# Due times of the last eight chunks, and issue and landing costs of transfers by their kind, in the planner of a two-layer transformer kernel

## The chip, the core and the metric

The kernel runs on one core of one Trainium2 chip. The metric is the device time of one execution in microseconds (us), smaller is better. A core has five engines with a queue each: PE (TensorE, the matrix engine), DVE (VectorE), ACT (ScalarE), POOL (GpSimd) and SP (SyncE), which here issues every DMA. Each engine works off its queue in order, so the order in which instructions are issued decides who waits for whom.

## The reference

The input is x of 8 sequences with 1024 rows of 256 numbers, all float32. Four blocks follow each other, each with a layernorm before it and a residual sum after it:

```python
x = x + decoder(_layernorm(x), ...)      # flow attention, 16 heads of 16; own residual, layernorms and
                                         # a feed-forward 256 -> 1024 -> 256 with gelu
x = x + relu(_layernorm(x) @ w1 + b1) @ w2 + b2          # 256 -> 1024 -> 256
t = _layernorm(x)                        # softmax attention over the whole sequence, one head of 256
Q, K, V = split(t @ W_qkv.T + b_qkv)
x = x + softmax(Q @ K.T / 16) @ V
t = fp4(_layernorm(x))                   # fp4: blocks of 16, scale = max/6, rounded to 8 magnitudes
x = x + fp4(silu(t @ fp4(w_gate).T) * (t @ fp4(w_up).T)) @ fp4(w_down).T     # 256 -> 704 -> 256
```

The flow attention is causal (running sums along the sequence). The softmax attention isn't: a row needs the keys of its whole sequence.

## The kernel before

Rows are handled in chunks of 128 (64 in all, 8 in each sequence) and in groups p of four chunks (16 in all, two in each sequence). `linear_attention` does the flow attention group by group, `dense` the two feed-forward layers, for which it streams the weights from HBM again for every group (`w_in`, `w_out`, tiles of 128 KB, five buffers each), `norms_1` and `norms_2` the layernorms between. `soft_chunk(cc)` does softmax attention and the fp4 layer for chunk cc (0 to 63): `n2T,wqk` (the query), four products `n2T,qT` (scores), `ident,prob` or `ident,flow` (transposes of the probabilities), `vt,probT`, then layernorm and fp4 rounding on DVE, `ident,n` (transposes), two pairs of `wgT,xqT` and `wuT,xqT`, SiLU and product into a tile of 704 columns (`hid`, or `q` and `k` where free buffers of those names are lent), the fp4 rounding of it on DVE with one square on ACT, `ident,hid` (transposes), `wdT,hqT`, the last sum `y` and the store.

The order of all this isn't written out by hand. While the program is built, every part is a Python generator that yields what its next step needs, and `Plan.run` picks among them. For that, `Plan.took` keeps a cost model of each queue: a cost by engine, operation and size, and, for a DMA, when it lands. `Plan.run` takes the step with the smallest key:

```python
key = wait, unripe, queue == "tensor", not stays, part[2]
```

`part[2]` is the due time `at`. It decides last, among steps that are as ready as each other. Due times are counted in groups: group p of the flow attention is due from p, `dense` from p + 1 to p + 2, chunk cc of `soft_chunk` from 3.5 + cc/4, with its transposes 0.25, 0.5 and 0.75 later. A chunk starts when its whole sequence is normed and fewer than eight chunks are in flight; at most three are between their scores and their `vt,probT` product.

When the model sees TensorE idle for more than 1.6 us, and a bank of PSUM is free, `Plan.run` calls `fill`, which puts products of the identity with itself (`bank<-ident`) into the gap, 0.22 us of them at a time, for the length of the gap less 0.7 us. One such product is two passes in the trace. Nothing reads them.

In the flow attention `spread` widens a small tile: two DMAs write `packed` (128 x 128) to HBM, then four (`flow`) or two (`scale`) read it back as `spread` tiles of 128 x 512. For every transfer the model had one cost, and one time to landing beyond that of its bytes:

```python
        else:
            cost = 0.4
...
            after = self.free["rings"] - end + 2.1
```

Every instruction goes through `Queue.issue` (the helper's line, L337 in the profile), so groups of instructions are told apart by their tiles and not by their lines.

Of the kernel before, what the change touches and what calls it, by code (L numbers as in the profile page):

```python
# [16 lines left out]
P = 128  # L17
# [45 lines left out]
class Plan:  # L63
# [96 lines left out]
    def took(self, queue, op, args, kw):  # L160

        aps = [x for x in list(args) + list(kw.values()) if isinstance(x, bass.AP)]
        outs = [kw["out"] if "out" in kw else aps[0]]
        if kw.get("accum_out") is not None:
            outs.append(kw["accum_out"])
        size = 1
        for ap in aps:
            n = 1
            for d in ap.shape[1:]:
                n *= d  # L170
            size = max(size, n)

        overlap, after = 0.0, 0.035
        if queue == "tensor":
            size = 1
            for d in outs[0].shape[1:]:
                size *= d
            cost = size * (0.853e-3 if op == "transpose" else 1.687e-3)
            tiled = op == "matmul" and (kw["lhsT"].shape[-1] <= 32 or kw["lhsT"].shape[0] <= 32)
            if tiled or op == "matmul" and kw["lhsT"].dtype == BF16:  # L180
                cost *= 0.25
            if tiled != self.tiled:
                cost += 0.2
            self.tiled = tiled
            after = 0.2
        elif queue == "vector":
            each = {"reciprocal": 6.2e-3, "tensor_tensor_scan": 2.15e-3}.get(op, 1.05e-3)
            cost = 0.17 + each * size
            if op == "tensor_scalar" and outs[0].dtype == BF16:
                cost = 0.16 + 0.26e-3 * size  # L190
            elif op == "scalar_tensor_tensor" and any(ap.shape[-1] == 1 for ap in aps):
                cost += 0.06
            overlap = 0.08
        elif queue == "scalar":
            cost = (0.16 if op == "copy" else 0.26) + 0.82e-3 * size
            for x in args:
                if not isinstance(x, bass.AP) and self.SETS.get(x, self.act_set) != self.act_set:
                    self.act_set = self.SETS[x]
                    self.free[queue] = self.free.get(queue, 0.0) + 1.3
            if kw.get("accum_out") is not None:  # L200
                cost += 0.15
            overlap = 0.1
        elif queue == "gpsimd":
            cost = 0.65 + 0.7e-3 * size
            if op in ("tensor_scalar", "iota"):
                cost = 0.22
            elif op == "memset":
                cost = 0.1 + 0.9e-3 * size
        else:
            cost = 0.4  # L210
        start = self.free.get(queue, 0.0)
        if queue not in ("tensor", "sync"):
            start = max([start] + [self.used.get(ap.tensor.name, 0.0) for ap in outs])
        for ap in aps:
            name = ap.tensor.name
            if self.by.get(name) != queue or queue in ("vector", "gpsimd"):
                start = max(start, self.done.get(name, 0.0) + (0.05 if queue == "gpsimd" else 0.0))
            if name not in self.done and name in self.held:
                start = max(start, self.used[name])
        if queue == "tensor":  # L220
            if start - self.ran > 2.0:
                self.slow = start + 2.1
            if start < self.slow:
                cost *= 2
            self.ran = start + cost
        if queue == "sync":
            start = max(start, self.landed.pop(0))
        end = start + cost
        if queue == "sync":
            n = 4e-6 / 250e-3  # L230
            for d in outs[0].shape:
                n *= d
            self.free["rings"] = max(self.free.get("rings", 0.0), end) + n
            after = self.free["rings"] - end + 2.1
            self.landed.append(end + after)
        self.free[queue] = end - overlap
        for ap in outs:
            self.done[ap.tensor.name] = end + after
            self.by[ap.tensor.name] = queue
        for ap in aps:  # L240
            name = ap.tensor.name
            self.used[name] = max(self.used.get(name, 0.0), end + after)
            if queue != "tensor" and name not in self.kept:
                self.held.discard(name)
# [11 lines left out]
    def pe(self, *tiles, **kw):  # L256
        return self.need("tensor", tiles, **kw)

    def dve(self, *tiles, **kw):
        return self.need("vector", tiles, **kw)  # L260
# [95 lines left out]
def block_stack_kernel(ctx: ExitStack, tc: tile.TileContext, a: dict, out: bass.AP):  # L356
# [20 lines left out]
    plan = Plan(tc, tc.nc)  # L377
    nc, pe, dve, act, dma = plan, plan.pe, plan.dve, plan.act, plan.dma
    x_dram = a["L0_attn_inputs"]
    B, L, _ = x_dram.shape  # L380
    NCH = L // P
# [1120 lines left out]
    def soft_chunk(cc):  # L1502
# [1 line left out]
        g, i = divmod(c, G)  # L1504
        q = seqs[s]
        n2T, vt = q["n2T"], q["vt"]
        at = 3.5 + cc / 4
        yield pe(
            banks=1,
            when=lambda: count["asked"] == cc  # L1510
# [130 lines left out]
    def softmax_and_fp4():  # L1641
        for cc in range(B * NCH):
            q = seqs[cc // NCH]
            yield dve(
                at=3.5 + cc / 4,
                when=lambda: q["normed"] == NCH and cc - count["out"] < (8 if plan.spare else 4) and "softmax" in weights and "ends" in late,
            )
            plan.start(soft_chunk(cc), 3.5 + cc / 4)

    def fill(us):  # L1650

# [7 lines left out]
    for part in (linear_attention(), masks(), late_constants(), zeros(), load_weights_and_rows(), dense(), softmax_and_fp4(), fp4_weights(), softmax_weights()):  # L1659
        plan.start(part, 0.0)  # L1660
# [43 lines left out]
```

## Time and profile before

| | |
|---|---|
| median of 3 runs | 2649.98 us (2648.61 to 2650.44) |
| the profiled execution's own time | 2649.28 us |
| its span, first to last instruction | 2647.6 us |
| mean granted TensorE clock | 0.999 |
| PE, DVE, ACT, POOL busy | 2610.0, 1927.3, 1308.1, 576.9 us |
| transfers of `w_in` and `w_out` | 1024 of 128 KB |
| transfers of `packed`, `spread` | 60 of 64 KB, 90 of 256 KB |

The profile is of one execution. Its own time is 1.68 us longer than its span and 0.70 us under the median of the runs. A line of a timeline has the start, the time, the engine, the operation, the tiles out<-in, the shape and the count, and in brackets the idle time before it with what ended it. A line of windows has the stretch, its length, and the busy time of each engine in it (with the count of instructions), then the granted TensorE clock, the share of DMA and GB/s.

### The profile page before, as it was taken

Reading aid. Unit: us, or ns where it says so; the run is one execution under the profiler, and the core shown is the slowest. Engines: PE = TensorE matmul, PEld = TensorE weight load, DVE = VectorE, ACT = ScalarE, POOL = GpSimd, SP = SyncE. Lnnn points to the kernel's source line nnn. Section 1 sums busy time; section 2 is a strip of 40 time slices with the busy share of each in tenths; the row PEclk is TensorE's granted clock in tenths of the full one; section 3 lists DMA queues with packets and bytes.
Section 4 is the critical chain, followed back from the end, with each engine's and each line's share of the span. In section 5 each row is a group of like instructions: output and inputs, shape, how many; then the busy total and the mean of one; then the engine's idle time right before and its main releaser. Section 6 shows DMA issues by size and latency. Waiting matters only on the chain.

```text
span 2647.6 us, 46665 instructions
## 1 busy us (share of the span) xinstructions
PE 2610.0 (99%) x16995; PEld 2043.8 (77%) x16995; DVE 1927.3 (73%) x4353; ACT 1308.1 (49%) x2671; POOL 576.9 (22%) x1101
## 2 busy tenths in 40 slices
PE   8999999999999999999999999999999999999999
PEld 7777787877778777787777778777787777777776
DVE  7888786868768586776868678586776867655676
ACT  4534445455464544536455364555536455453443
POOL 2333332212213122131222212122131222111000
PEclk9999999999999999999999999999999999999999
DMA  3435323223132232322323232232322323122000
GB/s 93 124 87 155 99 86 104 77 70 108 56 96 73 76 104 64 92 71 76 90 74 104 63 92 75 73 107 65 88 72 79 91 63 107 55 84 65 14 20 9
DMA packets 286821, 211.96 MB, mean 80 GB/s; under 512 B 24704, under 2 KB 275072, under 8 KB 286592
## 3 DMA queue, kind: packets, MB, share of 16 engines
q1 hardware_dynamic: 286592, 208.97, 27.4%
q8 instruction: 136, 2.23, 0.4%
q14 instruction: 93, 0.76, 0.1%
HBM read 188.17 MB, written 20.71 MB: 79 GB/s over the span
## 4 chain that ended last, share of the span: by engine, by line
PE 86%; DVE 7%; DMA 3%; ACT 3%; issue 1%; POOL 0%; SPq 0%; DVEq 0%; POOLq 0%; ACTq 0%
PE bank L337 86%; DVE prod L337 3%; DMA spread<-packed 2%; ACT L337 1%; DMA packed<-flow 1%; DVE spread L337 1%; DVE hid L337 1%; DVE ln_st L337 0%; ACT prob L337 0%; DVE r L337 0%; DVE u L337 0%; ACT n0T L337 0%; DVE n L337 0%; DVE res L337 0%; DVE ln_mv L337 0%
## 5 line engine op out<-in xcount | busy, mean ns | idle before, releaser
L337 PE MATMUL bank<-half,w_in 128*128 128x256 f32 x2048 | 530.6, 382 | 4.3 <-DMA w_in<-in_L_ffn_w_dram 1.4
L337 PE MATMUL bank<-w_out,hidden 128*128 128x256 f32 x2048 | 532.1, 383 | 0.2 <-ACT hidden L337 0.2
L337 POOL TENSOR_SCALAR ln_ve<-ln_mv 128x1 f32<-128x1 f32 x384 | 97.8, 255 | 1719.3 <-DVE ln_mv L337 1699.9
L337 PEld LDWEIGHTS bank<-w_out,hidden 128*128 128x128 f32 x2048 | 369.5, 190 | 92.7 <-issue 39.6
L337 PEld LDWEIGHTS bank<-half,w_in 128*128 128x128 f32 x2048 | 380.2, 191 | 77.5 <-issue 26.6
L337 ACT ACT_TABLE_LOAD x328 | 420.8, 1283 | 5.9
L337 ACT ACTIVATE hidden<-bank,c_L_ffn_b 128x256 f32<-128x256 f32 x256 | 122.0, 477 | 333.7 <-PE bank L337 333.7
L337 POOL TENSOR_TENSOR ln_rstd<-ln_ve,neghalf 128x1 f32<-128x1 f32 x384 | 237.0, 617 | 31.9
L337 PE MATMUL bank<-n2T,qT 128*128 128x512 f32 x512 | 241.8, 595 | 0.5 <-ACT qT L337 0.5
L337 PE MATMUL bank<-vt,probT 128*128 128x256 f32 x1024 | 231.3, 379 | 0.0
L337 PEld LDWEIGHTS bank<-vt,probT 128*128 128x128 f32 x1024 | 193.3, 190 | 27.0 <-issue 1.0
L337 ACT ACTIVATE hidden<-bank,c_L_attn_b 128x256 f32<-128x256 f32 x256 | 120.5, 471 | 186.7 <-PE bank L337 186.5
L337 DVE TENSOR_TENSOR hid<-hid,bank 128x352 f32<-128x352 f32 x116 | 60.0, 518 | 166.3 <-PE bank L337 138.2
L337 PE MATMUL bank<-wdT,hqT 128*128 128x256 f32 x768 | 176.4, 379 | 1.0 <-ACT hqT L337 1.0
L337 PE MATMUL bank<-wgT,xqT 128*128 128x352 f32 x512 | 172.7, 460 | 0.9 <-ACT xqT L337 0.9
L337 PE MATMUL bank<-wuT,xqT 128*128 128x352 f32 x512 | 172.3, 459 | 0.0
L337 PEld LDWEIGHTS bank<-wdT,hqT 128*128 128x128 f32 x768 | 145.4, 190 | 22.6 <-ACT hqT L337 1.4
L337 DVE TENSOR_TENSOR sc<-bank,triu 128x512 f32<-128x512 f32 x240 | 148.7, 680 | 8.3 <-PE bank L337 7.7
L337 PEld LDWEIGHTS bank<-n2T,qT 128*128 128x128 f32 x512 | 92.0, 190 | 65.9 <-issue 60.0
L337 PEld LDWEIGHTS bank<-wuT,xqT 128*128 128x128 f32 x512 | 97.3, 190 | 54.2
L337 PEld LDWEIGHTS bank<-wgT,xqT 128*128 128x128 f32 x512 | 94.2, 190 | 34.0 <-ACT xqT L337 1.4
L337 DVE TENSOR_REDUCE mx<-bank 128x1 f32<-128x512 f32 x128 | 86.0, 672 | 29.2 <-PE bank L337 29.2
(220 smaller groups left out, 4430.4 us busy)
## 6 DMA issues: line engine op xcount, KB each, us to landing
w_in<-in_L_attn_W_dram SPq DMA_DIRECT2D x256, 128.0 KB
w_out<-in_L_attn_W_dram SPq DMA_DIRECT2D x256, 128.0 KB
w_in<-in_L_ffn_w_dram SPq DMA_DIRECT2D x256, 128.0 KB
w_out<-in_L_ffn_w_dram SPq DMA_DIRECT2D x256, 128.0 KB
spread<-packed SPq DMA_DIRECT2D x90, 256.0 KB
x<-in_L_attn_inputs_dram SPq DMA_DIRECT2D x64, 128.0 KB
xr<-in_L_attn_inputs_dram SPq DMA_DIRECT2D x64, 128.0 KB
rows<-res SPq DMA_DIRECT2D x64, 128.0 KB
```

The source lines that it names most:

```text
L337: ins = method(*args, **kw)
```

## The change

Chunk cc of `soft_chunk` is due at 3.5 + min(cc, 56)/4 in place of 3.5 + cc/4, in all three places where the due time stands. The chunks 56 to 63, which are those of the last sequence, are therefore all due at 17.5 (before: 17.5 to 19.25), and so are, by stages, their transposes, 0.25, 0.5 and 0.75 later. In the cost model of a DMA, one that moves 512 or more elements in a partition, or that writes `packed`, costs 0.6 us of its queue, every other 0.38 (before: 0.4 for all), and one below 512 elements lands 1.5 us after its bytes (before: 2.1 for all). No instruction of the computation is added or taken away. The program is the planner's answer to these numbers.

```diff
@@ Plan.took
         else:
-            cost = 0.4
+            spreads = size >= 4 * P
+            cost = 0.6 if spreads or "packed" in outs[0].tensor.name else 0.38
...
-            after = self.free["rings"] - end + 2.1
+            after = self.free["rings"] - end + (2.1 if spreads else 1.5)
@@ soft_chunk
-        at = 3.5 + cc / 4
+        at = 3.5 + min(cc, B * NCH - 8) / 4
@@ softmax_and_fp4
             yield dve(
-                at=3.5 + cc / 4,
+                at=3.5 + min(cc, B * NCH - 8) / 4,
...
-            plan.start(soft_chunk(cc), 3.5 + cc / 4)
+            plan.start(soft_chunk(cc), 3.5 + min(cc, B * NCH - 8) / 4)
```

## The prediction

> **What bounds the kernel now.** I read the page's busy times first, then the windows, then the timelines of the two places where TensorE isn't full.
>
> ```profile
> span 2647.6 us, 46665 instructions
> PE 2610.0 (99%) x16995; PEld 2043.8 (77%) x16995; DVE 1927.3 (73%) x4353; ACT 1308.1 (49%) x2671; POOL 576.9 (22%) x1101
> ```
>
> TensorE is busy for all but 37.6 us, so the time is its work, plus its gaps, plus what it does for nothing. The groups of instructions have 292 passes of `bank<-ident`, 37.0 us, nearly all of it fill or warm-up. No order of issue can gain more than these two sums; what it can lose is open. The windows say where the gaps are:
>
> ```profile
> 100.00:300.00 200.00, 187.40 (x1470) 149.12 (x1469) 164.32 (x375) 86.65 (x207) 64.67 (x117) 0.98 0.41 118
> 137.00:152.00 15.00, 10.74 (x74) 8.35 (x73) 12.33 (x37) 4.43 (x12) 4.77 (x10) 0.77 0.19 60
> 300.00:2400.00 2100.00, 2092.95 (x13593) 1639.62 (x13592) 1524.15 (x3407) 1070.24 (x2140) 473.07 (x891) 1.00 0.29 83
> 2444.70:2587.30 142.60, 140.51 (x633) 102.39 (x632) 102.63 (x242) 67.37 (x131) 9.07 (x22) 1.00 0.06 19
> 2587.30:2647.60 60.30, 54.11 (x287) 42.17 (x285) 38.57 (x80) 20.52 (x39) 1.48 (x4) 1.00 0.03 10
> ```
>
> The first number after the stretch is PE. Between 300 and 2400 us it lacks 7.05 of 2100 us; there is nothing to win there. Between 100 and 300 it lacks 12.6. The last product of the dense layers (`w_out,hidden`) ends at 2444.7; in the 202.9 us from there it lacks 2.09 + 6.19 = 8.28, of which 3.25 lie behind the last matmul (2644.35). The timeline shows what the end is filled with:
>
> ```profile
> 2587.37 1.50 PE L337 MATMUL bank<-ident 128*128 128x128 f32 x12
> ...
> 2618.99 2.17 PE L337 MATMUL bank<-ident 128*128 128x128 f32 x18
> ...
> 2625.53 1.50 PE L337 MATMUL bank<-ident 128*128 128x128 f32 x12
> ...
> 2631.62 1.35 PE L337 MATMUL bank<-wuT,xqT 128*128 128x352 f32 x4
> 2632.81 7.08 PE L337 MATMUL bank<-ident 128*128 128x128 f32 x62
> 2640.16 0.87 PE L337 MATMUL bank<-ident,hid 128*128 128x128 f32 x6 [0.27 <-DVE hid L337]
> 2641.49 2.86 PE L337 MATMUL bank<-wdT,hqT 128*128 128x256 f32 x12 [0.46 <-ACT hqT L337]
> ```
>
> Here 104 passes, 12.25 us, are fill: TensorE has run out of other work while single chunks go through the fp4 rounding on DVE one after the other. The longest is the last chunk's, 7.19 us from the end of its `wuT` product (2632.97) to its transposes (2640.16).
>
> **The due times.** In the changed program's order of issue TensorE has 106 fill products instead of 146: the 52 at the end are gone, 12 more stand between the 159th and 213th row of its queue. With the due times alone its order is the old one up to the last sequence and the end has no fill; with the costs alone the end still has 47. So the two parts can be costed apart.
>
> After the last `w_out` product both programs issue the same matmuls (160 passes of `vt,probT`, 144 of `wdT,hqT`, 88 each of `wgT` and `wuT`, 178 transposes, and so on). The work of the end stays, and the stretch changes by fill and gaps alone. The fill goes: -12.2. What is late next is DVE. Of the 202.9 us DVE works 102.6 + 38.6 = 141.2, so it can't bind the whole stretch, but the scores now come early and the fp4 rounding late. I summed both queues from the last `vt` product of the new order to the end. PE: 8 pairs `wgT`/`wuT` at 2.37 (start to start, 2595.85 to 2598.22), 8 `wdT` at 2.59, two `ident,n` at 0.22, five sets of hidden transposes at 0.65: 43.4 us. DVE: five 704-column roundings at 5.45 (0.89 + 0.19 + 0.43 + 0.89 + 0.34 + 1.82 + 0.89, from 2633.63 on), eight products with the bank at 0.52, eight sums `y` at 0.42, one 256-column layernorm and rounding of 4.25: 39.1. TensorE still binds, by 4.3 us. Inside its chains DVE waits for ACT's square (0.86 in each) and POOL's `ln_rstd` (0.95): 5 x 0.86 + 0.95 + 0.48 = 5.7 if nothing stands between. So this stretch costs between nothing and 1.4 us from DVE's order.
>
> The last chunk's 7.19 us no longer lie bare: behind its last `wuT` the new order has eight transposes (0.22 + 0.44 + 0.22) and two `wdT` of other chunks (5.18), 6.1 us, and the wait left is 1.1. Then the wait of 0.46 for `hqT` as before. Before, the waits in this window were 4.8 (`hid` 1.7, `hqT` 1.0, `xqT` 0.9, `qT` 0.5, others 0.7). The planner finds no gap over 1.6 us that it can fill, so I expect several short ones, together 2.5, and 4 with the two named: -0.8. The end gives -13. Its bounds: -17.0 (fill and all waits), and 0 if each wait stays and only loses its fill.
>
> Against taking fill away speaks the clock. The row: after gaps of 1.60, 1.00 and 0.90 us within 5 us the granted clock was 0.77 over 137 to 152 us (second window), 15 x 0.23 = 3.5 us lost at most.
>
> ```profile
> 142.65 0.44 PE L337 MATMUL bank<-ident,w_raw 128*128 128x128 f32 x2 [1.60 <-DVE w_raw L337]
> 144.08 0.44 PE L337 MATMUL bank<-ident,n 128*128 128x128 f32 x2 [1.00 <-DVE n L337]
> 145.41 0.58 PE L337 MATMUL bank<-total,front 128*128 128x1 f32 x2 [0.90 <-ACT e L337]
> ```
>
> In the new end the gaps I count are 1.1 and less, with 2.6 us of work between them, so I price this at 0, and at +3.5 in the range. (The Trainium skill, "TensorE: Matmul & The Clock Gate", Part 1, lets the clock halve only after an idle window of about 3.4 us; by it the price is 0 here, and the row above, where no single gap was so long, doesn't agree with reading it as one gap.)
>
> **The costs of transfers.** These move only the plan. What they should say stands in SP's rows (shortest/median/longest in ns); the last line is TensorE's timeline:
>
> ```profile
> L337 SPq DMA_DIRECT2D spread<-packed x90: 543/586/1493, 122.0 to 2241.4; - x90
> L337 SPq DMA_DIRECT2D packed<-flow x30: 536/568/633, 117.7 to 2209.5; - x30
> L337 SPq DMA_DIRECT2D w_in<-in_L_attn_W_dram x256: 367/379/1017, 20.3 to 2355.7; - x128
> 129.74 1.13 PE L337 MATMUL bank<-half,w_in 128*128 128x256 f32 x4 [1.43 <-DMA w_in<-in_L_ffn_w_dram]
> ```
>
> The medians are 0.586, 0.568 and 0.379 us: 0.6 and 0.38 are nearer than 0.4. A round of two `packed` and four `spread` takes 6 x 0.18 = 1.1 us more of SP than the old plan thought, and DVE waited 33.5 us, in 19 waits, for `spread`. From 300 us on TensorE has work during these waits, so their end is worth at most part of the 7.05 us; I take 0, with 3 either way for the reshuffle.
>
> Before 300 us it can matter. In the fourth line above TensorE waits for a load of `w_in` that SP issued behind four `spread` (124.80, after 122.02 to 124.71); in the new order it stands ahead of them, and I take the 1.43 us as won. The `spread` then start one issue later (0.5 us), and their chain on DVE ends at `total,front` (145.41). There the plan has 13 fill products where it had 8 (10 passes more, 1.1 us) and moves two `ident,n` (0.44) and two `half,w_in` (1.73) ahead of `total,front`, into the gaps of 1.60 to 0.90. Some 50 rows later 7 new fill products (14 passes, 1.6 us) wait for `h`. Sum: -1.4 - 2.2 + 1.1 + 1.6 = -0.9, call it -1. Dozens of instructions change places in this region, so its bounds are wide: -8 (two thirds of the 12.6 us) to +8 (as much again).
>
> SP's queue itself: a load of `w_in` issued later delays the `hidden` chain only if five buffers at 1.73 us a step, 8.6 us, are used up; in 512 loads that was so once.
>
> **Sum.** Span 2647.6 - 13 - 1 + 0 = 2633.6; the execution's own time 1.7 more, 2635.3; the median of the runs was 0.7 above that execution, 2636.0. That is the forecast.
>
> **The rivals.** (1) DVE takes the fill's place. If half of the seven earlier chunks of the last sequence show their DVE waits bare (0.95 + 0.48 + 0.86 = 2.29 each, 8.0), and the last stretch its 1.4, 9.4 of the 13 are lost, and the time is about 2645. For it: DVE's share over the end is 70%, and it will be 90% (39.1 of 43.4) in the last part. Against: it was 83% at 2500 to 2550 (41.7 of 50.0 us) with TensorE full. (2) The change doesn't do what it says: fill goes, but each of its four gaps stays as plain idle time: 2636 + 13 = 2649. Against: the 6.1 us of other chunks' work that now stands in the longest. (3) Slower. The shorter landing (1.5) lets the planner leave `w_in` behind the four `spread` in every round, and TensorE waits as at 129.74: 1.43 us in each of the 15 rounds of `flow`, 21.5 in all: 2636 + 21.5 = 2658. It decides from 14 rounds on ((14 + 5.3)/1.43 = 13.5). Against: the buffers' 8.6 us, and one such wait in 512 loads.
>
> **How the numbers follow.** About 0.2%, 5.3 us, is what a measurement of this kernel can tell from no change. The forecast (2636; its own range 2625 to 2644) has 0.70, rival 1 0.15 (half of it below 2644.7), rival 2 0.07, rival 3 0.08. Faster: 0.70 + 0.08 = 0.78; same 0.07 + 0.07 = 0.14; slower 0.08. The range goes from 2625 (fill, half the waits and the early -8) to 2648, which leaves out rival 3 and most of rival 2.
>
> **What would show it.** Right: no `bank<-ident` after 300 us; under 5 us of PE idle between the last `w_out` product and the last matmul; the stretch from that product to the end near 190 us instead of 202.9; no wait of TensorE for `w_in` near 130. Wrong: a wait for `hid`, `n` or `hqT` over 2 us in the last 60 us, a granted clock under 0.95 there, or more than 20 us of PE idle before 300 us.

## The result, and the profile after

The changed kernel takes 2660.36 us (median of 5 runs, 2658.45 to 2661.03) against 2649.92 us before: a ratio of 1.0039, interval 1.0026 to 1.0052. It is slower by 0.4%, where 0.5% less was forecast. The profiled execution took 2660.36 us with a span of 2658.5. The page's busy times and, below them, its share of the chain that ended last:

```profile
span 2658.5 us, 46475 instructions
PE 2610.4 (98%) x16915; PEld 2035.0 (77%) x16915; DVE 1932.5 (73%) x4353; ACT 1272.5 (48%) x2638; POOL 566.2 (21%) x1101
...
PE 73%; DVE 20%; DMA 2%; ACT 2%; POOL 1%; issue 1%; SPq 0%; DVEq 0%; ACTq 0%; POOLq 0%
```

TensorE has 80 passes less than before (104 of fill are gone from the end, 24 more stand in the first 300 us), and is still busy for as long (2610.0 before); its idle time rose from 37.6 to 48.1 us. The windows, PE first after the stretch, the granted clock third from the end:

```profile
100.00:300.00 200.00, 190.72 (x1496) 151.22 (x1495) 166.19 (x381) 87.62 (x208) 63.70 (x116) 0.99 0.41 118
300.00:2400.00 2100.00, 2076.23 (x13459) 1617.63 (x13458) 1516.19 (x3361) 1028.48 (x2086) 457.33 (x877) 1.00 0.28 81
2472.50:2655.30 182.80, 180.64 (x815) 133.19 (x813) 138.81 (x315) 82.35 (x165) 8.95 (x24) 1.00 0.05 17
```

The place where nothing was to be won has lost: TensorE lacks 23.8 of 2100 us where it lacked 7.05. The starts of the `w_out,hidden` passes date the loss. The 257th starts at 288.2 us (288.7 before) and the last at 2472.19 (2444.45 before). From there to the end of the last matmul it is 183.1 us (199.9 before). So the early part gives -0.5, the middle +28.2 and the end -16.8: +10.9 of the 11.1 between the two profiled executions.

The middle's gaps have names. TensorE's waits, with their sum, number and longest; the last line is that of the kernel before:

```profile
PE bank L338 <- DVE sc L338: 11.7, 10, 2.0
PE bank L338 <- DVE v L338: 8.2, 17, 0.9
...
PE bank L337 <- DVE sc L337: 0.7, 1, 0.7
```

Before, TensorE had no listed wait for `v`. The same waits come back with every sequence, 324 us apart. This is one of the five longest, in TensorE's timeline and in DVE's:

```profile
858.50 0.38 PE L338 MATMUL bank<-ident,h 128*128 128x128 f32 x2
860.90 2.04 PE L338 MATMUL bank<-half,w_in 128*128 128x256 f32 x4 [2.02 <-DVE sc L338]
...
857.68 0.68 DVE L338 TENSOR_TENSOR sc<-bank,triu 128x512 f32<-128x512 f32 x1
858.28 0.86 DVE L338 TENSOR_TENSOR n<-n,q_c 128x256 f32<-128x256 f32 x1
859.18 0.42 DVE L338 TENSOR_TENSOR n<-n,x_s 128x256 f32<-128x256 f32 x1
859.52 0.73 DVE L338 TENSOR_SCALAR n<-res,ln_mv,ln_rstd 128x256 f32<-128x256 f32 x2
860.17 1.88 DVE L338 TENSOR_TENSOR sc<-bank,triu 128x512 f32<-128x512 f32 x3
```

`half,w_in` computes nothing from `sc`. It waits because it has been given a PSUM bank that still holds the second quarter of the scores, which DVE reads out at 860.17, after four other instructions. The built program lists the bank of every tile: both tiles have bank 3. The planner knew nothing of this. At each product it strikes off the bank that has been unused longest (`Plan.bank`) and reckons with that one, here a bank that was free before the product's start. The pool behind `mm_bank` hands out the bank, by an order of its own. The two differ in 632 of 2463 products in the changed kernel and in 539 of 2466 in the one before.

Whether that costs anything can be worked out from the program and the planner's clock alone: how long before the last reader of its bank is done does each product start by plan? Below these are called hidden waits. The kernel before has 5 of them, 1.1 us in sum; the changed kernel 48, 31.9 us.

### The profile page after: what moved, and what is told of

Read it like the earlier page. It is cut to its first block, busy times and chain, and to the rows that moved or that the text cites. A ratio compares the mean times of both kernels' runs of the same rounds, so it can differ in the third digit from the quotient of the medians.

```text
span 2658.5 us, 46475 instructions
## 1 busy us (share of the span) xinstructions
PE 2610.4 (98%) x16915; PEld 2035.0 (77%) x16915; DVE 1932.5 (73%) x4353; ACT 1272.5 (48%) x2638; POOL 566.2 (21%) x1101
## 4 chain that ended last, share of the span: by engine, by line
PE 73%; DVE 20%; DMA 2%; ACT 2%; POOL 1%; issue 1%; SPq 0%; DVEq 0%; ACTq 0%; POOLq 0%
PE bank L338 73%; DVE prod L338 3%; DVE hid L338 2%; DVE n L338 2%; DVE ln_st L338 1%; DMA spread<-packed 1%; DVE res L338 1%; DVE spread L338 1%; DVE u L338 1%; DMA packed<-flow 1%; DVE div L338 1%; DVE ln_mv L338 1%; ACT L338 1%; DVE x_amax L338 1%; DVE mx L338 1%
## 5 line engine op out<-in xcount | busy, mean ns | idle before, releaser
L338 POOL TENSOR_TENSOR ln_rstd<-ln_ve,neghalf 128x1 f32<-128x1 f32 x384 | 233.2, 607 | 31.9
```

Of the source, the lines that this page charges most:

```text
L338: ins = method(*args, **kw)
```

## The experiments

**The two parts apart.** The first kernel takes back the costs, the second the due times.

```diff
 first:
-            cost = 0.6 if spreads or "packed" in outs[0].tensor.name else 0.38
+            cost = 0.4
-            after = self.free["rings"] - end + (2.1 if spreads else 1.5)
+            after = self.free["rings"] - end + 2.1
 second, in its three places:
-        at = 3.5 + min(cc, B * NCH - 8) / 4
+        at = 3.5 + cc / 4
```

> The due times alone, with transfers counted at 0.4 us and a landing of 2.1 us as before. Up to the last sequence TensorE's order is the old one, at the end there is no fill. If the two parts simply add, the middle (300 to 2400 us) is as before, the stretch behind the last w_out product is some 17 us shorter, and the time is 2650 - 17 = 2633 us (2630 to 2637). If the loss in the middle has anything to do with the due times, it is above 2640 us.

> The costs of transfers alone, with the old due times. TensorE's order is that of the changed kernel up to the last sequence, and the end has fill again (47 products). If the two parts add, the middle loses the same 27 us and the end is as before: 2650 + 27 = 2677 us (2671 to 2681), with the same waits of half,w_in for DVE sc of about 2.0 us, once a sequence. If the loss needs both parts, the time is within 5 us of 2650.

The due times alone took 2636.71 us, 0.9958 [0.9945, 0.9970] of the kernel before; the costs alone 2677.70, 1.0114 [1.0100, 1.0128]. Against the 2648.73 of the kernel before on that chip they are -12 and +29; their sum of +17 is 7 above the change's +10, and 4.2 of that is the end, which is shorter with both (183.1 us) than with the due times alone (187.3). The loss belongs to the costs alone. The first was expected at 2633 (2630 to 2637): alone, the due times give 12.6 us at the end (187.3 instead of 199.9), not 17. The second came where it was expected (2671 to 2681) and has the same waits for `sc` (11.7 us) and `v` (9.4).

**The banks apart.** The third and fourth kernel change no instruction and no order on any engine. They are the changed kernel and the due times alone, with each bank a pool of one buffer, so that a product gets the bank the planner reckons with.

```diff
+    def place(self):
+        if len(self.banks) < BANKS:
+            return len(self.banks)
+        old = min((b for b in self.banks if b not in self.held), key=lambda b: self.used[b])
+        return self.at[old]
...
-        bank = ps.tile([P, 512], F32, tag="bank", name="bank")
-        plan.bank(bank)
+        k = plan.place()
+        bank = ps.tile([P, 512], F32, tag=f"bank{k}", name="bank", bufs=1)
+        plan.bank(bank, k)
```

> The changed kernel with the same order of instructions on every engine; only the PSUM bank of each product is another: each of the eight banks is a pool of its own, and the product takes the bank that the planner reckons with (in the changed kernel the pool hands out a bank of its own choice; for the product that waits 2.02 us at 858.70 it is the bank of the second scores quarter, which DVE still has to read, where the planner counted on a bank that was free). Theory A, the middle's loss is such banks: TensorE's waits for DVE sc (11.7 us) and DVE v (8.2 us) and the half-clock passes behind them go, and the time is 2660 - 20 to 27 = 2633 to 2640 us. Theory B, DVE is late by its own order and any bank would have had to wait: within 5 us of 2660.

> The due times alone, and the planner's bank for each product; the order on every engine is that of the due times alone. Theory A: the old order has few waits for banks in the middle (TensorE lacks 7 of 2100 us there), so this gains at most these 7 us and some at the end: 2625 to 2633 us, up to 7 us below the due times alone. Theory B: the same as the due times alone within 2 us.

The changed kernel with the planner's banks took 2626.54 us, 0.9918 [0.9904, 0.9931]: 33.8 us less than with the pool's banks, and the best version found here. That is 6.5 us below the range of theory A (2633 to 2640): the cause is borne out, the gain was put too low. The due times alone with the planner's banks took 2633.94, 0.9945 [0.9932, 0.9959], 2.8 us less than with the pool's banks: between the two expectations, and the runs of the two kernels overlap, so this one decides nothing. The third kernel's page, its windows and one row of its waits:

```profile
span 2624.5 us, 46504 instructions
PE 2595.7 (99%) x16915; PEld 2030.6 (77%) x16915; DVE 1932.4 (74%) x4353; ACT 1270.2 (48%) x2638; POOL 563.7 (21%) x1101
...
300.00:2400.00 2100.00, 2096.69 (x13616) 1641.58 (x13615) 1530.35 (x3400) 1038.28 (x2111) 461.89 (x891) 1.00 0.28 83
800.00:1124.00 324.00, 323.97 (x2103) 253.04 (x2102) 240.83 (x536) 161.44 (x332) 71.16 (x138) 1.00 0.28 82
...
PE bank L346 <- DVE sc L346: 0.5, 3, 0.2
```

Over one sequence, 324 us, TensorE now lacks 0.03 us. The 16915 passes are the same as in the changed kernel, so the 33.8 us can be split: idle time fell by 19.3 us (48.1 to 28.8) and busy time by 14.7 (2610.4 to 2595.7). Part of the 14.7 is the clock: the changed kernel's execution has five stretches of 3.41 us at half clock, the third kernel's none (the last section shows them). Compared pass by pass, these stretches account for 8.2 us. Most of the other 6.5 lies right beside the gaps, where passes that take 0.38 us and otherwise start 0.22 us apart no longer overlap. The expectation had the waits right and this busy time too small. DVE's busy time is equal (1932.5 and 1932.4): it was not too slow, it was asked for the wrong bank.

The Trainium skill ("Perfetto Trace Analysis", Optimization Strategy) says that the same gap repeating on the engine that should be saturated can mean that there isn't enough PSUM for the next tile. The gap of 2.02 us, repeated every 324 us, is of this kind; but eight banks are enough here, since with the same eight and the same order the gaps are gone.

**Is it the cost's size?** If banks decide, then neither a right nor a wrong cost should matter by itself. Four kernels with the due times and another cost for `spread` and `packed`; the seventh is the sixth's order with the planner's banks, the eighth has them too. The fifth to seventh also keep the old 0.4 and the landing of 2.1 for the other transfers.

```diff
-            cost = 0.6 if spreads or "packed" in outs[0].tensor.name else 0.38
+            cost = 0.58 if spreads or "packed" in outs[0].tensor.name else 0.4    # fifth
+            cost = 0.8 if spreads or "packed" in outs[0].tensor.name else 0.4     # sixth, seventh
+            cost = 0.61 if spreads or "packed" in outs[0].tensor.name else 0.38   # eighth
```

> The due times, and 0.58 us instead of 0.6 for spread and packed (0.4 and 2.1 for the rest, as before), with the pool's own banks. Two numbers come out of the planner and the built program: the end of the plan (2613.3 us on the planner's clock; the changed kernel 2610.3) and the hidden waits, the sum over all products of how long before the bank's last reader is done, by the planner's clock, the product is planned to start (8.7 us; the changed kernel 31.9, the kernel before 1.1). Theory A, the loss is the banks: the changed kernel with the planner's banks took 2626.5; 3.0 more for the plan and 8.7 to 9.5 for the hidden waits give 2638 us (2633 to 2643). Theory C, a higher cost for spread and packed is what slows the middle, wherever the banks are: 2657 to 2661, as 0.6 did.

> The due times, and 0.8 us for spread and packed, a cost that is clearly too high (the rows have 0.568 and 0.586), with the pool's own banks. Planner's clock 2615.0, hidden waits 42.6 us. Theory A: 2626.5 + 4.7 + 42.6 to 45 = 2674 to 2676 us (2668 to 2680). A theory by which the time follows the accuracy of the costs, or by which the changed kernel's order was one bad draw, gives no such number; it would expect some 2640 to 2660.

> The same order on every engine as with 0.8 us, but each product in the bank that the planner reckons with: no hidden waits. Theory A: 2626.5 + 4.7 = 2631 us (2627 to 2636), 42 us or more below the run with the pool's banks, though the cost of 0.8 is wrong. If the too high cost itself costs time, above 2640.

> The changed kernel with the planner's banks and 0.61 us instead of 0.6 for spread and packed. No hidden waits, but the plan is another one: it ends at 2635.6 us on the planner's clock (2610.3 with 0.6), and has 23.6 us of TensorE idle between 300 and 2300 us (4.3 with 0.6). If the plan's clock tells the time once the banks are its own, the time is 2626.5 + 25.3 = 2652 us (2645 to 2657), so that 0.01 us in one cost is worth 25 us by the luck of a greedy order. If the banks were all there was, 2627 us within 4.

With 0.58 it took 2638.97 us, 0.9962 [0.9947, 0.9977]: as theory A says, and 21 us away from the 0.6 of the changed kernel, so a higher cost for `spread` and `packed` is not by itself what slows it (the numbers of the other transfers differ as well). With 0.8 and the planner's banks it took 2632.53, 0.9938 [0.9923, 0.9952], again as expected, though that cost is far too high.

With 0.8 and the pool's banks it took 2653.55, 1.0019 [1.0009, 1.0029]: the banks cost 21.0 us, not 42.6. The sign held, the size didn't, and 2653.55 lies in the range that the expectation gave to other theories (2640 to 2660). The number alone doesn't decide then; the pair does, since the order is the same in both. The sum counts too much where hidden waits come in a row: once TensorE has waited, the products behind it start late by themselves, and DVE has caught up. Taking only the longest of each group (waits less than 6 us apart) gives 20.6 us for this order and 20.4 for the changed kernel's. Measured as idle time of TensorE the banks cost 17.1 us here (50.2 against 33.1) and 19.3 there. This rule was made after the run; that it fits the changed kernel too is some support, no test.

With 0.61 and the planner's banks it took 2644.68, 0.9988 [0.9978, 0.9997]: 18 us more than with 0.6, where the plan's clock said 25 (2645 to 2657 was expected, and 2627 if banks were all there was). No bank is wrong here, the order itself is worse, and the planner sees it: 23.6 us of idle time in its own plan's middle. So a hundredth of a microsecond in one cost is worth 18 us here, by the order that follows from it.

**The two remaining corners.** The kernel before, and the costs alone, with the planner's banks (the diff of the third kernel).

> The kernel before, same order on every engine, each product in the bank that the planner reckons with. Its hidden waits are 1.1 us on the planner's clock, in two places; the longest of each place add up to 0.6. Theory A: 2649 - 0.6 to 1.1, within 3 us of 2649. If another bank by itself makes products faster, as much as in the changed kernel (34 us): 2615.

> The costs alone with the planner's banks; up to the last sequence the order of the changed kernel, and the old due times at the end. Theory A: the same 33.8 us less than the costs alone as the changed kernel gained (2660.4 to 2626.5): 2677.7 - 33.8 = 2644 us (2640 to 2648); the costs alone are then a gain of some 5 us on the kernel before with its planner's banks, and the loss is wholly the banks'. If the costs have a loss of their own, above 2650.

They took 2646.27, 0.9991 [0.9982, 1.0000], and 2644.33, 0.9983 [0.9974, 0.9992]. Both are as theory A says, the first within its 3 us. All together, in us (the kernel before took 2648.5 to 2649.9 beside them):

| order of issue | pool's banks | planner's banks | hidden waits, sum |
|---|---|---|---|
| before | 2648.5 | 2646.3 | 1.1 |
| due times alone | 2636.7 | 2633.9 | 1.8 |
| costs alone | 2677.7 | 2644.3 | 31.9 |
| both (the change) | 2660.4 | 2626.5 | 31.9 |
| due times, 0.8 | 2653.6 | 2632.5 | 42.6 |

With the planner's banks the change is a gain of 19.7 us in place of a loss of 10.4: -12.3 for the due times, -1.9 for the costs, and -5.5 more for both together.

## Why the prediction was wrong

**The step that failed** is the middle: "From 300 us on TensorE has work during these waits, so their end is worth at most part of the 7.05 us; I take 0, with 3 either way for the reshuffle". It cost 28.2, of which 16.7 are idle time of TensorE. The 3 us for the reshuffle had no working behind it. The 7.05 us bound what could be won, and I let them bound what could be lost as well, although the text says of the loss that it "is open". The planner's order was known to change over 2100 us, and an order says nothing of the banks until one looks up which tile got which bank. With the planner's banks the same order takes 2150.1 us for the stretch that took 2155.8 before and 2184.0 with the pool's: the order itself was a gain of 5.7 us. The 31.9 us of hidden waits could have been counted beforehand, from the built program and the planner's own clock.

**The costs did what they say.** DVE's waits for `spread` fell from 33.5 us to 20.4 (the first two lines are before, the others after):

```profile
DVE spread L337 <- DMA spread<-packed: 32.0, 17, 3.0
DVE q L337 <- DMA spread<-packed: 1.5, 2, 1.1
...
DVE spread L338 <- DMA spread<-packed: 18.7, 12, 3.0
DVE q L338 <- DMA spread<-packed: 1.7, 3, 1.1
```

That this alone would win little was right, 1.9 us with the planner's banks; beside the due times the costs win 7.4 there.

**The end held.** I forecast -13; the due times alone gave -12.6, and with the costs -16.8, mostly since that order has fewer waits (2.2 us of idle time between the last `w_out` product and the last matmul, against 5.5). No fill stands after 300 us. The two waits named in the sum are there as forecast, 1.1 for `hid` and 0.46 for `hqT`; the further short ones, put at 2.5, came to 0.6:

```profile
2651.10 0.87 PE L338 MATMUL bank<-ident,hid 128*128 128x128 f32 x6 [1.13 <-DVE hid L338]
2652.43 2.86 PE L338 MATMUL bank<-wdT,hqT 128*128 128x256 f32 x12 [0.46 <-ACT hqT L338]
```

The clock's price of 0 in this stretch held too (1.00 in the third window above).

**The early part** came to -0.5 by the 257th `w_out` pass where -1 was forecast, and TensorE's wait for `w_in` near 130 is gone. The number proves little: in four executions with the old order there (the kernel before and the due times alone, each with either kind of banks) this pass started at 288.7, 287.7, 289.0 and 287.0 us. And the clock, which had no term here, moved too: over 137 to 152 us it was 0.77 before and 1.00 after, and it was at half from 178.31 to 181.72 us instead.

**The signs.** All four signs of being right came (the stretch behind the last `w_out` product took 186.0 us), and none of being wrong, though the time was missed: none of them looked between 300 and 2400 us.

**The rivals.** The first two did not occur: the fill's time was won, with no gap left in its place and no DVE chain shown bare. The third had the sign and the chance of 0.08, but not the mechanism: TensorE waits for no `w_in` after 300 us. Its 15 waits of 1.43 us were sought at a queue; the real ones, 27 for `sc` and `v`, came from who owns a bank. That 2658 and 2660 are so near is luck.

## What to carry to other kernels

A planner that orders instructions by a model needs every choice that ends in a wait to be its own: if it reckons with one buffer and an allocator hands out another, its order is tuned to a machine that doesn't exist, and each new order draws new waits. So when a change reorders a full engine, count before running it how many products are planned to start before their buffer's last reader is done, by group; and if a better cost model makes a kernel slower, fix the model's blind spot before taking the cost back. An engine that is 99% busy has little to win in its middle, and everything to lose there.

## What the hardware showed

The same gap halves the clock at one time and not at another. Four of the five repeats of the wait for `sc` in the changed kernel, TensorE's timeline, with the rows behind two of them:

```profile
1184.84 1.73 PE L338 MATMUL bank<-half,w_in 128*128 128x256 f32 x4 [2.03 <-DVE sc L338]
1186.36 0.64 PE L338 MATMUL bank<-ident,hid 128*128 128x128 f32 x2
1186.79 1.91 PE L338 MATMUL bank<-w_out,hidden 128*128 128x256 f32 x4
...
1508.70 1.33 PE L338 MATMUL bank<-half,w_in 128*128 128x256 f32 x4 [2.02 <-DVE sc L338]
...
1832.22 1.13 PE L338 MATMUL bank<-half,w_in 128*128 128x256 f32 x4 [2.02 <-DVE sc L338]
1833.19 0.38 PE L338 MATMUL bank<-ident,hid 128*128 128x128 f32 x2
1833.41 1.03 PE L338 MATMUL bank<-w_out,hidden 128*128 128x256 f32 x4
...
2154.85 1.13 PE L338 MATMUL bank<-half,w_in 128*128 128x256 f32 x4 [2.02 <-DVE sc L338]
```

Four `half,w_in` passes take 2.04 us after the gap at 860.90, 1.73, 1.33 and then twice 1.13: the slow clock sets in with the first pass, the second, the fourth, or not at all. The work around them is the same each time; what differs is when the gap falls. The granted clock falls to half five times in the changed kernel's execution, at 178.31, 393.35, 860.97, 1185.24 and 1509.51 us, each time for 3.41 us, and the distances are 63, 137, 95 and 95 times 3.413 us. On this grid, the stretch with the gap and the one behind it, for the first, fourth and fifth repeat:

```profile
857.56:860.97 3.41, 1.39 (x10) 0.95 (x7) 3.38 (x8) 1.23 (x3) 1.30 (x2) 1.00 0.28 83
860.97:864.38 3.41, 3.41 (x9) 2.75 (x10) 3.20 (x9) 0.80 (x2) 0.98 (x4) 0.50 0.03 9
1830.36:1833.77 3.41, 1.54 (x8) 1.37 (x9) 3.34 (x9) 0.63 (x3) 0.00 (x0) 1.00 0.14 43
1833.77:1837.18 3.41, 3.41 (x21) 3.02 (x20) 2.44 (x8) 1.76 (x6) 2.38 (x6) 1.00 0.31 86
2151.21:2154.62 3.41, 1.62 (x11) 1.17 (x9) 3.38 (x8) 1.40 (x3) 1.51 (x3) 1.00 0.38 106
2154.62:2158.03 3.41, 3.18 (x19) 2.83 (x20) 3.20 (x10) 1.45 (x5) 0.77 (x3) 1.00 0.13 38
```

Where the whole gap lay in one stretch, TensorE was busy for 1.39 us of it, and the next had half the clock; the second and third repeat are alike (1.38 and 1.39). Where the grid cut the gap, TensorE was busy for 1.54 and 1.62 us, and the clock stayed. Busy time alone doesn't decide, though: ahead of 178.31 and 393.35 it was 2.95 and 1.95 us, with other passes, and the clock fell all the same.

The Trainium skill ("TensorE: Matmul & The Clock Gate", Part 1) has the gate judge by a window of about 3.4 us that runs freely. That it runs freely agrees with these rows; that the window has to be idle does not, as no gap near these rows is over 2.03 us. What else the gate counts these runs don't tell. Nor was it tried why the pool chooses as it does.
